# Cross-attention and quantised feed-forward on one core: the shape of the reads, of the first loads and of the warm-up

## The chip, the cores and the metric

The kernel runs on one core of a Trainium2 chip. The metric is the device time of one execution in microseconds (us). A core has five engines with a queue of instructions each: TensorE (PE in the profile, its weight loads PEld), VectorE (DVE), ScalarE (ACT), GpSimd (POOL) and SyncE (SP). SyncE computes nothing here; it issues DMAs. DMAs issued by SyncE, ScalarE and GpSimd are carried out by 16 DMA engines that the queues share.

## The reference

`x` and `ctx` are 4 x 1024 x 512 floats. Normalisation, biases and all weights are as below; the attention has 16 heads of 32, and a mask by blocks: 768 image tokens attend within three chunks of 256, and 256 text tokens attend to all image tokens and causally to text.

```python
qh = heads(layernorm(x) @ Wq + bq); kh = heads(ctx @ Wk + bk); vh = heads(ctx @ Wv + bv)
scores = where(mask, einsum('bhqd,bhkd->bhqk', qh, kh) * 32 ** -0.5, -inf)
x = x + merge(softmax(scores) @ vh) @ Wo + bo

xq = fake_quant(layernorm(x), clip_x)            # one scale for the whole tensor, 8 bits
gate, up = xq @ fq(w_gate).T, xq @ fq(w_up).T    # 512 -> 1408, weights by rows, 8 bits
h = fake_quant(silu(gate) * up, clip_down)
x = x + h @ fq(w_down).T
```

## The kernel before

Tokens are cut into 16 blocks of 256 (`QB`), four to a batch element: three image blocks and one text block. Two kinds of job are done for each block: `kv` (its context turned so that features lie on partitions, then K and V) and `q` (normalised x turned, then Q). A large loop (L984) goes over *units*: an image block has 4 units, one for each group of four heads; a text block has 16, one for each group and each quarter of the keys. The order of units and jobs is written out by hand, and the order on PE, DVE, ACT and POOL is the order of the code (`manual_schedule`, L923). SyncE's queue alone is ordered by the scheduler of the framework.

**Image units of the first three batch elements (36 of them, `rows`)** compute their scores with queries on partitions. `maxima` (L456) makes scores and their maxima, `exponents` (L492) the exponentials E and their sums, `quotients` (L508) divides on GpSimd. The weights must then be turned so that keys lie on partitions. This goes through DRAM and VectorE: `send_out` (L514) stores E, 128 partitions of 8 KB, in a DRAM tile `e_d`; `fetch` (L519) reads it back into the tile `S` in another arrangement; `turned` (L525) transposes 32 x 32 blocks of S on VectorE (L530); `row_values` (L532) multiplies by V. In the iteration of unit n, the loop fetches unit n - 2 (L998), stores unit n - 1 (L1000), then issues the posts (among them the store of normalised x, L400), the loads for the next small step (`prepare_next`, L1003) and the load of x1 for an output (`xr`, L137 by way of L1008), and transposes unit n - 3 (L1012). E and S have two buffers each. A fetch is four DMAs of 256 KB: each fills 32 partitions, with four rows of 2 KB on each.

Other image units and all text units compute scores a second time with keys on partitions (`weights`, L581), and need no such turn. Image stages with the round trip through DRAM lie at about 45 to 211, 318 to 449 and 552 to 690 us.

**Contexts.** `load_spread` (L143) reads a context block so that one VectorE transpose by blocks (L280) turns it: for image blocks by `mixed=True`, eight DMAs, each with 32 partitions by 4 runs of 512 bytes; for text blocks and for normalised x four DMAs with 32 partitions by 8 runs. The first context block is loaded by `load_mixed` (L154) and turned on TensorE against the identity (L291), with copies out on ScalarE (L292).

**Start.** After 14 warm-up products (L174, 128 x 512 each) come the loads: first context block, Wk in four chunks by `ci` (L178, each 128 partitions by 512; two on SyncE's queue and two on ScalarE's), biases on ScalarE's queue, the first x block, then Wv and Wq in four DMAs each of 32 partitions by 4 rows (L185), all on SyncE's queue.

**Background.** `statistics`, `deviation`, `apply` normalise an x block, and `largest`, `quantise` quantise a feed-forward weight. They stand in a deque, of which each iteration takes one at L1026, and one more after a `quantise` (L1029). After attention, the feed-forward stage (from about 985 us) has its own loops (L1287, L1359).

Of the kernel before, what the change touches and what calls it, by code (L numbers as in the profile page):

```python
# [10 lines left out]
F32 = mybir.dt.float32  # L11
# [8 lines left out]
P = 128  # L20
B, N, C = 4, 1024, 512
NH, D = 16, 32
FF = 1408
NCC = C // P
NIC = FF // P
QB = 256
NQB = N // QB
# [15 lines left out]
def kernel(ctx: ExitStack, tc: tile.TileContext, x, kv, Wq, bq, Wk, bk, Wv, bv, Wo, bo, clip_x, clip_down, w_gate, w_up, w_down, out):  # L43
    nc = tc.nc
    x_tok = x.rearrange("b n c -> (b n) c")
    kv_tok = kv.rearrange("b n c -> (b n) c")
# [11 lines left out]
    ident = cpool.tile([P, P], F32, tag="ident", name="ident")  # L58
# [3 lines left out]
    ones = cpool.tile([P, P], F32, tag="ones", name="ones")  # L62
# [58 lines left out]
    with ExitStack() as actx:  # L121
# [20 lines left out]

        def load_spread(src, c, mixed=False):  # L143
            t = ld.tile([P, NQB * 2, P], F32, tag="cb", name=f"spread_{c}")
            for i in range(NCC):
                to, cols = t[i * D : (i + 1) * D], slice(i * P, (i + 1) * P)
                if not mixed:
                    nc.sync.dma_start(to, src[:, cols].rearrange("(k q) m -> q k m", q=D))
                    continue
                for n in range(2):  # L150
                    nc.sync.dma_start(to[:, n * 4 : (n + 1) * 4], src[:, cols].rearrange("(g n q) m -> n q g m", n=2, q=D)[n])
            return t

        def load_mixed(src, c):  # L154
            t = ld.tile([P, 2, C], F32, tag="cb", name=f"cb_{c}")
            for g in range(4):
                rows = src[c * QB + g * 2 * D : c * QB + (g + 1) * 2 * D, :]
                nc.sync.dma_start(t[g * D : (g + 1) * D], rows.rearrange("(n q) c -> q n c", q=D))
            return t

        brow = ap.tile([3 * NCC, P], F32, tag="brow", name="brow")
# [9 lines left out]

        idle = ps_mm.tile([P, 512], F32, tag="mm", name="idle")
        rhs = onesb.unsqueeze(1).to_broadcast([P, 4, P])
        for _ in range(14):  # L174
            nc.tensor.matmul(idle.rearrange("p (a b) -> p a b", a=4), onesb, rhs, start=True, stop=True)
        cb0 = load_mixed(kv_tok, 0)
        for ci in range(NCC):
            (nc.sync if ci % 2 == 0 else nc.scalar).dma_start(W["Wk"][:, ci, :], Wk.rearrange("(i k e) f -> k i e f", k=NCC, e=D)[ci])  # L178
        for i, bias in enumerate((bq, bk, bv)):
            nc.scalar.dma_start(brow[i * NCC : (i + 1) * NCC, :], bias.rearrange("(c p) -> c p", p=P))  # L180
        nc.scalar.preload_act_table_set("natural_log_exp_and_others")
        xb0 = load_block(x_tok, 0, "xb")
        for name, w in (("Wv", Wv), ("Wq", Wq)):
            for i in range(NCC):
                nc.sync.dma_start(W[name][i * D : (i + 1) * D], w[i * P : (i + 1) * P, :].rearrange("(k e) f -> e k f", e=D))  # L185

        def other_loads():
            nc.sync.dma_start(W["Wo"], Wo.rearrange("(c p) f -> p c f", p=P))
# [40 lines left out]


        Q, K, V = {}, {}, {}
        xbs, spreads = {0: xb0}, {}

        early = [True]

# [28 lines left out]
        class Job:  # L264


            def __init__(self, kind, c, a):
                self.kind, self.c, self.a = kind, c, a
                self.small, self.big, self.part = 0, 0, 0
                self.smalls = 2 if c == 0 else 1  # L270
                self.bigs = 4 if kind == "kv" else 2

            def run_small(self):
                if self.small == 0:
                    self.T = wk2.tile([P, NCC, QB], F32, tag="tT", name=f"{self.kind}T_{self.c}")
                i = self.small
                self.small += 1
                if self.c > 0:
# [4 lines left out]
                if self.kind == "q":  # L283
                    while not ready.get(self.c):
                        background.popleft()()
                src = cb0 if self.kind == "kv" else xb0
# [6 lines left out]
                if i == 1 and self.kind == "kv":  # L293
                    columns_of_biases()
                elif i == 1:
                    next_queries(self.c)

            def rows(self, dst, w, b, scale, co, parts):
# [215 lines left out]
        def send_out(u):  # L514

            u.through = dram.tile([P, 8 * QB], F32, tag="e_d", name=f"e_d_{u.n}", bufs=4)
            nc.sync.dma_start(u.through, u.e.rearrange("p g n h x k -> p (g n h x k)"))

        def fetch(u):  # L519

            u.spread = t = bp.tile([P, 4, 2, QB], F32, tag="S", name=f"S_{u.n}")
            for g in range(4):
                nc.sync.dma_start(t[g * D : (g + 1) * D].rearrange("p b n f -> p b (n f)"), u.through.rearrange("(b q) (g f) -> g q b f", q=D, g=4)[g])

        def turned(u):  # L525

# [282 lines left out]
        def small_step():  # L809
            nonlocal at_small  # L810
            jobs[at_small].run_small()
            if jobs[at_small].small == jobs[at_small].smalls:
                at_small += 1
# [145 lines left out]
                posts.popleft()()  # L959

        small_step()
        small_step()
        send(2)
        take = jobs[0].first_rows()
        stage()
# [18 lines left out]
        for n in range(len(units) + V_LAG):  # L984
# [450 lines left out]
```

## Time and profile before

| | us |
|---|---|
| median of 3 runs | 1268.04 (1264.88 to 1270.05) |
| the profiled execution | 1271.16 |
| its span in the profile | 1269.3 |
| PE busy | 1112.7 (88%) |
| DVE busy | 788.8 (62%) |
| ACT busy | 558.7 (44%) |
| POOL busy | 539.1 (42%) |
| moved by DMA | 214.72 MB, 158832 packets |

Times in the profile count from the span's start. In the slices of a page, each digit is the busy share of one fortieth of the span, in tenths. The DMA share is the mean over the 16 engines, so 0.25 is four engines busy all the time, or sixteen for a quarter of it. A line such as "L523 SPq" is the queue of SyncE at line 523, and "to landing" runs from the issue of a DMA to the completion that others wait for. Engines wait on semaphores in the order of their queue: a waiting instruction holds everything behind it on its engine.

### The profile page before, as it was taken

To read this page: it belongs to the slowest core of one execution; us is meant where nothing else is said; L and a number is where in the kernel's file an instruction comes from. 1 tells how busy PE (TensorE), PEld (TensorE's weight loads), DVE (VectorE), ACT (ScalarE), POOL (GpSimd) and SP (SyncE) were. 2 spreads that over 40 slices of the span, in tenths; PEclk is the share of its full clock that TensorE was granted. 3 is DMA by queue.
4 is the path that set the end of the run, shared out by engine and by line. 5 is a ranking of instruction groups with operands and counts; after the bars stand their busy time and mean duration, and the time that the engine had idled before them with its cause. 6 is when DMAs were issued, how large, how long until landed. Compare 5 with 4: busy or idle time off the path is not lost.

```text
span 1269.3 us, 30483 instructions
## 1 busy us (share of the span) xinstructions
PE 1112.7 (88%) x12891; PEld 534.4 (42%) x12891; DVE 788.8 (62%) x1086; ACT 558.7 (44%) x1205; POOL 539.1 (42%) x542
## 2 busy tenths in 40 slices
PE   6977486989989798998988899999989894999898
PEld 4533232444443334454333445555544442344344
DVE  0435456745467784645678565585666784687797
ACT  1555241335754323486351344453434452544453
POOL 1334240468954316887351486675662221100010
PEclk7998697989999997998999999999989898899899
DMA  6599789945798962559798654211311399520595
GB/s 149 176 263 237 221 230 270 260 97 92 242 242 235 277 161 50 121 176 255 215 255 243 153 102 104 73 49 55 118 41 57 115 263 185 105 58 17 215 383 206
DMA packets 158832, 214.72 MB, mean 169 GB/s; under 512 B 49756, under 2 KB 99944, under 8 KB 152680
## 3 DMA queue, kind: packets, MB, share of 16 engines
q1 hardware_dynamic: 136200, 170.83, 49.5%
q0 software_dynamic: 22208, 41.42, 12.7%
q8 instruction: 101, 1.65, 0.6%
q10 hardware_dynamic: 288, 0.53, 0.1%
q14 instruction: 35, 0.29, 0.1%
HBM read 120.59 MB, written 90.70 MB: 166 GB/s over the span
## 4 chain that ended last, share of the span: by engine, by line
PE 37%; DVE 6%; DMA 5%; POOL 3%; issue 2%; ACT 2%; SPq 0%; DVEq 0%; POOLq 0%; ACTq 0%
PE pg L1275 5%; PE pu L1275 5%; PE pd L1378 4%; PE po L239 4%; PE pv L239 3%; PE av L642 3%; PE pp_q L239 2%; PE t L595 2%; PE s L479 2%; POOL sp L621 2%; DMA wdT<-wdq 2%; DMA xqT<-xq 2%; PE pp_kv L239 1%; PE s L468 1%; PE av L661 1%
## 5 line engine op out<-in xcount | busy, mean ns | idle before, releaser
L621 POOL TENSOR_TENSOR sp<-sp,pT 128x1024 f32<-128x1024 f32 x84 | 188.9, 2249 | 43.2 <-ACT pT L604 39.9
L512 POOL TENSOR_TENSOR E<-E,sums 128x1024 f32<-128x1024 f32 x72 | 135.7, 1893 | 153.0 <-DVE sums L510 105.6
L490 DVE TENSOR_REDUCE nmh<-s 128x2 f32<-128x1024 f32 (+1 forms) x128 | 145.1, 1155 | 56.1 <-PE s L479 53.9
L499 ACT ACTIVATE E<-s,nmh 128x256 f32<-128x256 f32 x288 | 132.7, 481 | 86.1 <-DVE nmh L472 37.0
L472 DVE TENSOR_REDUCE nmh<-s 128x4 f32<-128x1024 f32 x96 | 112.6, 1214 | 87.9 <-PE s L468 87.9
L600 ACT ACTIVATE pT<-t 128x1024 f32<-128x1024 f32 x76 | 78.0, 1027 | 200.3 <-PE t L595 196.8
L239 PE MATMUL pp_kv<-kvT,Wk_sb 128*32 128x256 f32 x1920 | 119.5, 400 | 18.3 <-DVE xr L695 18.1
L239 PE MATMUL pv<-Wv_sb,kvT 128*32 128x512 f32 (+1 forms) x1088 | 123.0, 587 | 4.8 <-DMA spread_kv<-in_ctx_dram 3.4
L239 PE MATMUL po<-Wo_sb,oT 128*32 128x512 f32 (+1 forms) x1056 | 114.4, 573 | 10.4 <-DVE xr L695 9.0
L239 PE MATMUL pp_q<-qT,Wq_sb 128*32 128x256 f32 x2048 | 121.9, 388 | 0.0
L1275 PE MATMUL pg<-xqT,wgT 128*128 128x512 bf16 x352 | 92.8, 388 | 21.2 <-DMA xqT<-xq 20.4
L1302 DVE SCALAR_TENSOR_TENSOR h<-pu,su,silu 128x512 f32<-128x512 f32 x88 | 65.4, 747 | 54.4 <-PE pu L1275 53.4
L1281 ACT ACTIVATE silu<-pg,sg 128x512 f32<-128x512 f32 x88 | 59.9, 686 | 89.0 <-PE pg L1275 89.0
L543 PE MATMUL av<-pT,va 128*32 128x256 f32 x576 | 48.4, 427 | 50.6 <-DVE pT L530 37.8
L1275 PE MATMUL pu<-xqT,wuT 128*128 128x512 bf16 x352 | 92.3, 386 | 0.0
L239 PEld LDWEIGHTS pp_kv<-kvT,Wk_sb 128*32 128x32 f32 x1920 | 62.4, 115 | 68.8 <-DVE xr L695 18.5
L530 DVE STREAM_TRANSPOSE pT<-S 128x1024 f32<-128x1024 f32 x72 | 85.0, 1218 | 6.2 <-DMA S<-e_d 6.2
L239 PEld LDWEIGHTS pp_q<-qT,Wq_sb 128*32 128x32 f32 x2048 | 64.5, 112 | 52.7 <-issue 9.8
L642 PE MATMUL av<-pT,va 128*32 128x256 f32 (+1 forms) x1216 | 80.5, 376 | 6.3 <-POOL pT L609 5.5
L479 PE MATMUL s<-kT,qT 32*128 32x256 f32 (+1 forms) x1024 | 82.2, 405 | 4.1 <-ACT pT L600 2.5
L595 PE MATMUL t<-qT,kT 32*128 32x256 f32 (+1 forms) x1216 | 80.4, 377 | 0.0
L604 ACT ACTIVATE pT<-t 128x1024 f32<-128x1024 f32 x76 | 78.0, 1027 | 0.0
(198 smaller groups left out, 1590.5 us busy)
## 6 DMA issues: line engine op xcount, KB each, us to landing
e_d<-E SPq DMA_DIRECT2D x36, 1024.0 KB, 5.9
S<-e_d SPq DMA_DIRECT2D x144, 256.0 KB, 6.4
xt<-x_d SPq DMA_DIRECT2D x16, 1024.0 KB, 8.0
h<-h_d POOLq DMA_DIRECT2D x3, 2816.0 KB, 13.4
xb<-in_x_dram SPq DMA_DIRECT2D x16, 512.0 KB, 7.6
x_d<-bo_b SPq DMA_DIRECT2D x16, 512.0 KB, 9.1
x_d<-in_x_dram POOLq DMA_DIRECT2D x16, 512.0 KB, 7.6
xr<-x_d SPq DMA_DIRECT2D x16, 512.0 KB, 5.2
```

Source lines behind the costliest of these rows:

```text
L239: nc.tensor.matmul(out[rows_of(j)], lhs[:, rows_of(j)], rhs, start=start, stop=stop, tile_position=(0, j * D), skip_group_check=True)
L472: nc.vector.tensor_reduce(nmh[:, h, :, :, 0], prs[h], AX.X, ALU.max, negate=True)
L479: nc.tensor.matmul(prs[j // 2][:, j % 2, kk, :w], q[rows_of(j), g, i * P : (i + 1) * P], K[k.keys[2 * half + kk]][rows_of(j), g, :w], star ...
L490: nc.vector.tensor_reduce(nmh[:, h, :, i, half], s[:, :, :n], AX.X, ALU.max, negate=True)
L499: nc.scalar.activation(u.e[:, :, :, h, x, :].rearrange("p g n k -> p n g k"), u.s[h][:, jj, i, :].rearrange("p (n g k) -> p n g k", n=2, g=4),
L512: nc.gpsimd.tensor_tensor(e, e, u.sums[h].unsqueeze(1).unsqueeze(3).to_broadcast([P, 8, 4, D]), ALU.mult)
L530: nc.vector.transpose(pT[:, n], u.spread[:, :, n].rearrange("p b (y k) -> p b y k", k=D))
L595: nc.tensor.matmul(prs[j // 2][:, j % 2, n, cols], kc[rows_of(j), g, n * P : (n + 1) * P], q[rows_of(j), g, cols], start=False, stop=(n == 1))
L600: nc.scalar.activation(pT[:, :2], prs[0], AF.Exp)
L621: nc.gpsimd.tensor_tensor(sp[:, :, cols], a, pT[:, :, n, cols], ALU.add)
L642: nc.tensor.matmul(av[rows_of(j), 0, cols], va[:, n, g * P + j * D : g * P + (j + 1) * D], u.pT[:, j, n, cols], start=(u.part == 0 and n = ...
L1275: nc.tensor.matmul(ps, w[:, ic, cc, :], qT[:, cc, :], start=(cc == 0), stop=(cc == NCC - 1))
```

## The change

1. `fetch` reads S in four DMAs by b in place of four by g. Each still has 128 rows of 2 KB; it fills all 128 partitions with one row each, where it was 32 partitions with four rows each.
2. `load_spread(mixed=True)` likewise: eight DMAs of 128 partitions with one run of 512 bytes. The first context block is now loaded by it and turned by VectorE like the others; `load_mixed`, its products and its copies are gone, and `columns_of_biases` is called from the start of the schedule.
3. Wk comes in four chunks on ScalarE's queue; Wv and Wq in four chunks each, in turn on SyncE's and ScalarE's queues, all in the form that Wk had.
4. The warm-up has 10 of the large products, and then 7 rounds of 16 small ones on 32 x 32 tiles (256 columns in four rounds, 64 in three).
5. In the loop, `send_out` comes after the posts, `prepare_next` and the load of x1.
6. One more background step is taken in an iteration when it is `statistics` or `largest`, and more wait.

SyncE's queue, as the scheduler orders it, changes with this: where it sometimes had two stores of E in a row and then two fetches, store and fetch now alternate nearly everywhere, and in the first image stage the load of the next x block stands ahead of that of x1.

```diff
         def load_spread(src, c, mixed=False):
             t = ld.tile([P, NQB * 2, P], F32, tag="cb", name=f"spread_{c}")
-            for i in range(NCC):
-                to, cols = t[i * D : (i + 1) * D], slice(i * P, (i + 1) * P)
-                if not mixed:
-                    nc.sync.dma_start(to, src[:, cols].rearrange("(k q) m -> q k m", q=D))
-                    continue
-                for n in range(2):
-                    nc.sync.dma_start(to[:, n * 4 : (n + 1) * 4], src[:, cols].rearrange("(g n q) m -> n q g m", n=2, q=D)[n])
+            if mixed:
+                for k in range(NQB * 2):
+                    n, g = k // 4, k % 4
+                    at = (2 * g + n) * D
+                    nc.sync.dma_start(t[:, k], src[at : at + D, :].rearrange("q (i m) -> i q m", i=NCC))
+            else:
+                for i in range(NCC):
+                    nc.sync.dma_start(t[i * D : (i + 1) * D], src[:, i * P : (i + 1) * P].rearrange("(k q) m -> q k m", q=D))
...
-        for _ in range(14):
+        for _ in range(10):
             nc.tensor.matmul(idle.rearrange("p (a b) -> p a b", a=4), onesb, rhs, start=True, stop=True)
-        cb0 = load_mixed(kv_tok, 0)
-        for ci in range(NCC):
-            (nc.sync if ci % 2 == 0 else nc.scalar).dma_start(W["Wk"][:, ci, :], Wk.rearrange("(i k e) f -> k i e f", k=NCC, e=D)[ci])
+        tiles = [ps_sc.tile([P, 2, 2, QB], F32, tag="sc", name=f"idle_{h}") for h in range(2)]
+        for rounds, n in ((4, QB), (3, 2 * D)):
+            for _ in range(rounds):
+                for k in range(4):
+                    for j in range(4):
+                        nc.tensor.matmul(
+                            tiles[j // 2][k * D : (k + 1) * D, j % 2, 0, :n].rearrange("p (a b) -> p a b", b=2 * D),
+                            ident[j * D : (j + 1) * D, k * D : (k + 1) * D],
+                            ones[j * D : (j + 1) * D, : 2 * D].unsqueeze(1).to_broadcast([D, n // (2 * D), 2 * D]),
...
+        def load_weight(name, w, queues):
+            for ci in range(NCC):
+                queues[ci % len(queues)].dma_start(W[name][:, ci, :], w.rearrange("(i k e) f -> k i e f", k=NCC, e=D)[ci])
+
+        first = {0: load_spread(kv_tok[:QB, :], "kv_0", True)}
+        load_weight("Wk", Wk, [nc.scalar])
...
-        for name, w in (("Wv", Wv), ("Wq", Wq)):
-            for i in range(NCC):
-                nc.sync.dma_start(W[name][i * D : (i + 1) * D], w[i * P : (i + 1) * P, :].rearrange("(k e) f -> e k f", e=D))
+        load_weight("Wv", Wv, [nc.sync, nc.scalar])
+        load_weight("Wq", Wq, [nc.sync, nc.scalar])
...
             u.spread = t = bp.tile([P, 4, 2, QB], F32, tag="S", name=f"S_{u.n}")
-            for g in range(4):
-                nc.sync.dma_start(t[g * D : (g + 1) * D].rearrange("p b n f -> p b (n f)"), u.through.rearrange("(b q) (g f) -> g q b f", q=D, g=4)[g])
+            for b in range(4):
+                nc.sync.dma_start(t[:, b].rearrange("p n f -> p (n f)"), u.through.rearrange("(b q) (g f) -> b g q f", q=D, g=4)[b])
...
                 fetch(before)
-            if previous is not None and previous.rows:
-                send_out(previous)
             for post in [posts.popleft() for _ in range(len(posts))]:
                 post()
             prepare_next(n)
...
                         o.load()
+            if previous is not None and previous.rows:
+                send_out(previous)
...
+            extra = background.popleft() if f is not None and len(background) > 1 and background[0].__name__ in ("statistics", "largest") else None
...
-            if f is not None:
-                f()
+            for stage_ in (f, extra):
+                if stage_ is not None:
+                    stage_()
```

More of the change, by code (lines that the diff above doesn't have):

```diff
@@ L144, in load_spread @@
             t = ld.tile([P, NQB * 2, P], F32, tag="cb", name=f"spread_{c}")
-            for i in range(NCC):
-                to, cols = t[i * D : (i + 1) * D], slice(i * P, (i + 1) * P)
-                if not mixed:
-                    nc.sync.dma_start(to, src[:, cols].rearrange("(k q) m -> q k m", q=D))
-                    continue
-                for n in range(2):
-                    nc.sync.dma_start(to[:, n * 4 : (n + 1) * 4], src[:, cols].rearrange("(g n q) m -> n q g m", n=2, q=D)[n])
-            return t
-        def load_mixed(src, c):
-            t = ld.tile([P, 2, C], F32, tag="cb", name=f"cb_{c}")
-            for g in range(4):
-                rows = src[c * QB + g * 2 * D : c * QB + (g + 1) * 2 * D, :]
-                nc.sync.dma_start(t[g * D : (g + 1) * D], rows.rearrange("(n q) c -> q n c", q=D))
+            if mixed:
[6 more added lines that the diff above has]
+                    nc.sync.dma_start(t[i * D : (i + 1) * D], src[:, i * P : (i + 1) * P].rearrange("(k q) m -> q k m", q=D))
             return t
@@ L173 @@
         rhs = onesb.unsqueeze(1).to_broadcast([P, 4, P])
-        for _ in range(14):
+        for _ in range(10):
             nc.tensor.matmul(idle.rearrange("p (a b) -> p a b", a=4), onesb, rhs, start=True, stop=True)
-        cb0 = load_mixed(kv_tok, 0)
-        for ci in range(NCC):
-            (nc.sync if ci % 2 == 0 else nc.scalar).dma_start(W["Wk"][:, ci, :], Wk.rearrange("(i k e) f -> k i e f", k=NCC, e=D)[ci])
+        tiles = [ps_sc.tile([P, 2, 2, QB], F32, tag="sc", name=f"idle_{h}") for h in range(2)]
[7 more added lines that the diff above has]
+                            ones[j * D : (j + 1) * D, : 2 * D].unsqueeze(1).to_broadcast([D, n // (2 * D), 2 * D]),
+                            start=True,
+                            stop=True,
+                            tile_position=(j * D, k * D),
+                            skip_group_check=True,
+                        )
+        def load_weight(name, w, queues):
[3 more added lines that the diff above has]
+        load_weight("Wk", Wk, [nc.scalar])
         for i, bias in enumerate((bq, bk, bv)):
@@ L231 @@
         Q, K, V = {}, {}, {}
-        xbs, spreads = {0: xb0}, {}
+        xbs, spreads = {0: xb0}, first
         early = [True]
@@ L269, in __init__ @@
                 self.small, self.big, self.part = 0, 0, 0
-                self.smalls = 2 if c == 0 else 1
+                self.smalls = 2 if c == 0 and kind == "q" else 1
                 self.bigs = 4 if kind == "kv" else 2
@@ L277, in run_small @@
                 self.small += 1
-                if self.c > 0:
+                if self.c > 0 or self.kind == "kv":
                     src = spreads.pop(self.a)
@@ L281, in run_small @@
                     return
-                if self.kind == "q":
+                if True:
                     while not ready.get(self.c):
                         background.popleft()()
-                src = cb0 if self.kind == "kv" else xb0
+                src = xb0
                 pt = bank(f"pt_{self.kind}_{self.c}_{i}").rearrange("p (a b) -> p a b", a=NCC)
@@ L292, in run_small @@
                 nc.scalar.copy(self.T[:, :, i * P : (i + 1) * P], pt)
-                if i == 1 and self.kind == "kv":
-                    columns_of_biases()
-                elif i == 1:
+                if i == 1:
                     next_queries(self.c)
@@ L521, in fetch @@
             u.spread = t = bp.tile([P, 4, 2, QB], F32, tag="S", name=f"S_{u.n}")
-            for g in range(4):
-                nc.sync.dma_start(t[g * D : (g + 1) * D].rearrange("p b n f -> p b (n f)"), u.through.rearrange("(b q) (g f) -> g q b f", q=D, g=4)[g])
+            for b in range(4):
+                nc.sync.dma_start(t[:, b].rearrange("p n f -> p (n f)"), u.through.rearrange("(b q) (g f) -> b g q f", q=D, g=4)[b])
         def turned(u):
@@ L961 @@
         small_step()
-        small_step()
+        columns_of_biases()
         send(2)
```

## The prediction

> **What bounds the kernel now.** I read the page's slices first, for where the DMA engines are full; then windows over the three stretches in which image units run; then windows over the first 21 us, where both shapes of load stand apart; then the queue totals; then the two lines that store E and fetch S; last SyncE's timeline in one image stage.
>
> From the page, busy time, slices and one queue (slices are 31.7 us):
>
> ```profile
> PE 1112.7 (88%) x12891; PEld 534.4 (42%) x12891; DVE 788.8 (62%) x1086; ACT 558.7 (44%) x1205; POOL 539.1 (42%) x542
> ...
> DMA  6599789945798962559798654211311399520595
> GB/s 149 176 263 237 221 230 270 260 97 92 242 242 235 277 161 50 121 176 255 215 255 243 153 102 104 73 49 55 118 41 57 115 263 185 105 58 17 215 383 206
> ...
> q10 hardware_dynamic: 288, 0.53, 0.1%
> ```
>
> TensorE is the busiest, but in slices 2 to 6, 11 to 13 and 18 to 21 the DMA engines reach 8 or 9 tenths at only 220 to 277 GB/s, while slice 39 moves 383 GB/s. Those are the stages in which the image units' weights go through DRAM (E stored, S fetched). Windows over them (after PE, PEld, DVE, ACT and POOL: granted clock, DMA share, GB/s):
>
> ```profile
> 45.00:211.00 166.00, 117.30 (x1546) 52.06 (x1546) 82.88 (x120) 69.96 (x253) 55.87 (x52) 0.86 0.85 239
> 345.00:445.00 100.00, 83.98 (x1104) 35.98 (x1100) 68.97 (x96) 44.40 (x161) 45.65 (x36) 0.97 0.93 251
> 570.00:690.00 120.00, 104.13 (x1316) 45.25 (x1314) 81.32 (x112) 54.12 (x188) 54.25 (x40) 0.93 0.89 242
> ```
>
> No compute engine is as full there as DMA: 85, 93 and 89%. The image stages have no room for dearer transfers. What the two shapes cost is seen at the start:
>
> ```profile
> 5.00:7.00 2.00, 1.11 (x6) 0.29 (x3) 0.00 (x0) 0.20 (x1) 0.00 (x0) 1.00 0.26 96
> 9.00:11.00 2.00, 0.00 (x0) 0.00 (x0) 0.00 (x0) 0.00 (x0) 0.00 (x0) 0.50 0.26 97
> 16.00:21.00 5.00, 5.00 (x24) 4.08 (x23) 0.00 (x0) 0.00 (x0) 0.00 (x0) 1.00 1.07 187
> ```
>
> In the first two, chunks of Wk load (L178, 128 partitions by 512 elements, 256 KB each). With several outstanding on two queues only 0.26 of 16 engines, about four, are busy, at 97 GB/s: 24.2 GB/s for each. In the third, Wv and Wq load by L185 (32 partitions by 4 by 512): all 16 engines are busy, but at 187 GB/s, 11 GB/s each. The 32-partition form stretches its packets; the 128-partition form runs them at full pace on a quarter of the engines. The line of q10 (ScalarE's queue) says it again: two chunks of 128 rows and three biases of 4 rows make 268 packets of data; the other 20 are completions, four for each of five transfers.
>
> The two lines of the round trip, and SyncE in the second image stage:
>
> ```profile
> L523 SPq DMA_DIRECT2D S<-e_d x144: 302/430/1864, 60.0 to 677.9; - x144
> ...
> DMA to landing us min/median/max: 3.3/6.4/9.7
> ```
>
> ```profile
> L517 SPq DMA_DIRECT2D e_d<-E x36: 320/338/891, 54.5 to 668.4; - x36
> ...
> DMA to landing us min/median/max: 4.2/5.9/9.2
> ```
>
> ```profile
> 382.96 0.34 SPq L517 DMA_DIRECT2D e_d<-E  x1
> ...
> 391.61 0.35 SPq L517 DMA_DIRECT2D e_d<-E  x1
> 392.08 4.20 SPq L523 DMA_DIRECT2D S<-e_d  x4
> ...
> 400.98 1.73 SPq L523 DMA_DIRECT2D S<-e_d  x4
> 405.70 0.34 SPq L517 DMA_DIRECT2D e_d<-E  x1
> ```
>
> 36 units each store 1 MB and fetch it back in four reads. By SyncE's issues the twelve stores of a stage run from 54.5 to 185.5, 318.3 to 432.3 and 552.0 to 668.4 us: 11 intervals of 131, 114 and 116 us, so 11.9, 10.4 and 10.6 us a unit.
>
> **The change part by part.**
>
> *The S fetch.* Count, bytes and row length stay (4 reads of 128 rows of 2 KB). The source, written (g q) f, now begins with g = 4 and the target with 128 partitions: exactly the shape of a Wk chunk, whose row is therefore the nearest. Each read goes over four engines, and as chunks outstanding together kept 0.26 busy, I take the same four for all reads. Each then carries 262 KB a unit: 262/24.2 = 10.8 us. Now a fetch takes every engine 4.8 us (512 packets over 16 engines at 150 ns, the packet records' median between 345 and 445 us).
>
> The Trainium skill speaks on both sides. "Trainium Kernel Development and Optimization", section Best Practices, says to tile always to 128 partitions; by that alone a fetch would run on 16 engines, 65.5/24.2 = 2.7 us, and the sum would be rival B. "DMA: Bandwidth & Descriptors", section "Why a DMA increments its semaphore by 16 and not by 1", says that the engines are the largest number up to 16 that divides the outermost size of both sides, here 4 and 128, and that this queue takes the lowest-numbered ones; by that the sum is mine. The Wk rows decide for the second.
>
> *Load of one of the four engines, a unit.* Besides S: the E store over 16 engines, 65.5/24.2 = 2.7 us. The rest from the windows: 0.85 x 166 = 141 us for 12 fetches, 0.93 x 100 = 93 for 10, 0.89 x 120 = 107 for 10; less 4.8 for each fetch and 2.7 for each store leaves 4.2, 1.8 and 3.2 us a unit (x, xn, x1, weights). The context loads take the same shape (8 reads, 512-byte rows, 27 ns a packet): 256 packets x 27 = 6.9 us on four engines in place of 1.7 on all; three such in the first stage and one in each other: 1.3, 0.5, 0.5 us a unit. Sums: 19.0, 15.8 and 17.2 us.
>
> *The chain.* On SyncE the changed order is store n+1, fetch n+1, store n+2 in strict turn for nearly all units. Fetch n+1 waits for store n+1, whose part on the four engines stands behind fetch n. So a unit is at least 10.8 + 2.7 + 1.5 us, the last from landing to SyncE's next first packet (0.4 from the last packet of the store at 143.4 to its landing, 1.1 from the issue at 60.0 to the first packet). That is 15.0 with no other traffic, and with all of it in line 20.5, 17.3 and 18.7. The load gives 19.0, 15.8, 17.2; half the 1.5 us gap will not be filled, so I take 19.8, 16.5, 18.0. Times 11: 218 + 182 + 198 = 598 us against 361: **+237**. The median slack between S landing and its transpose (L530) is some 9 us; that hides one late fetch, not a rate.
>
> *Store behind posts, prepared loads and xr (L1006 to L1016).* It puts xb's load ahead of the store. In the first stage VectorE waits 32.9 us for xb and SyncE 22.1 us over the run for x1's accumulation (ahead of xr). With the four engines full the gain is covered by them: 0. Bounds -33 and +22; the store and its fetch now stand behind xr's wait.
>
> *Start.* The four engines carry context 6.9, Wk, Wv and Wq 10.8 each, x 1.4: 40.7 us from the first packet at 1.8 us, so Wq lands at some 43 to 44 us. The query products now start at 37.8; the first finds its last chunk 6 us later: **+6**. Bounds -3 (two products fewer before it) and +10. The 32 KB bias loads' queue place, the transpose that moves from TensorE to VectorE, and the warm-up (4 of 14 products of 0.36 us out, 112 small ones in; 64 transposes on 32 columns, two passes each, took 3.6 us, so some 6 to 10) lie under these loads: 0, at worst +2 if the warm-up outlasts the context.
>
> *One more background step an iteration.* Statistics and weight maxima come earlier on VectorE, 62% busy; no count changes. 0; at most ±5, since TensorE is 283 of 295 us busy between 690 and 985 and cannot use it.
>
> Sum: the profiled execution took 1271.2 us (span 1269.3), 0.25% above the median of 1268.0. 1271 + 237 + 6 = 1514, on the median's scale **1510 us**.
>
> **Rivals.**
> A. The same, and SyncE's waits in line add up: the 22.1 us for x1 repeat with slower landings (+22), start +10, chain at its full 20.5, 17.3, 18.7 (+20): some 1560. For it: SyncE issues in order. Against: most loads are due well ahead.
> B. Other side, faster: reads of 128 partitions spread over all 16 engines. A fetch falls from 4.8 to 2.7 us, the 32.9 us wait for xb goes: 1268 - 33 = 1235. It decides if a fetch occupies more than about seven engines, since 1 MB must pass within the 4.8 us of now beside the store. For it: stretched packets do vanish. Against: 0.26 and 20 completions.
> C. Only the chain binds: other traffic falls into its gaps, 15.0 a unit: 495 - 361 = +134, so 1400. Against: the load alone is above it in every stage.
> D. Hidden: four engines, but S is needed late: 1268. The slack must grow every unit; it can't, since 15 is over 10.6.
>
> **How the numbers follow.** Forecast 0.62, A 0.15, B 0.08, C 0.12, D 0.03. Range 1410 to 1590: from just above C to past A; B, D and half of C are out. A measurement of this kernel tells 0.5% (6 us) from no change; faster 0.08, same 0.02, slower 0.90.
>
> **What the profile after would show.** Right: in the image stages GB/s falls to some 150 to 170 and DMA share to about 0.5, with S fetches landing after 11 us and more; VectorE's wait for S before L530 (6.2 us in all) becomes the longest wait; stores 16 to 20 us apart; text and feed-forward stages unchanged. At the start, share 0.26 to 0.4 until 40 us. Wrong: S landing within 6 us and share of 0.8 there would be B. The forecast fails if Wk's four engines are due to something other than its shape.

## The result: 1511 us, and where the 240 us lie

| | us |
|---|---|
| before, median of 4 runs | 1268.21 (1264.88 to 1270.05) |
| after, median of 4 runs | 1510.77 (1505.47 to 1517.22) |
| ratio after / before | 1.1918, 95% interval 1.1864 to 1.1973 |
| span in the profile, before and after | 1269.3 and 1507.3 |

The change makes the kernel slower by 19%. The kernel before has two levels, and all its runs in this table are on the upper one, while in the experiments (on three chips) most of its runs lie between 1234 and 1254 us, with a few at 1258 to 1272 that the comparisons leave out; there the whole change measures 1.2188 (1.2131 to 1.2245).

From the page of the kernel after, busy time, slices (now of 37.7 us) and the queue of ScalarE:

```profile
PE 1174.4 (78%) x13025; PEld 550.2 (36%) x13047; DVE 794.8 (53%) x1087; ACT 556.6 (37%) x1203; POOL 540.5 (36%) x542
...
DMA  2435666574445434453553444745201314971386
GB/s 102 156 142 174 183 197 228 160 188 94 101 151 143 149 143 160 146 117 82 143 150 137 157 147 171 169 115 101 79 15 38 109 41 139 269 199 29 110 328 239
...
q10 hardware_dynamic: 1080, 2.10, 0.4%
```

The compute engines are busy for about as long as before (TensorE 62 us longer, at a lower granted clock in the image stages), but each for a smaller share of the time. In the image stages, DMA shares of 8 and 9 tenths are gone, and the rate is 137 to 197 GB/s, with 228 in one slice, where it was 220 to 277. Windows over the three image stages say it with sharper edges (after PE, PEld, DVE, ACT and POOL: granted clock, DMA share, GB/s):

```profile
66.00:276.00 210.00, 126.51 (x1402) 50.29 (x1398) 76.34 (x109) 63.19 (x231) 51.44 (x48) 0.78 0.55 183
405.00:609.00 204.00, 131.03 (x1476) 55.56 (x1468) 79.66 (x111) 67.46 (x228) 70.96 (x57) 0.79 0.46 149
732.00:933.00 201.00, 133.82 (x1478) 56.11 (x1468) 79.67 (x111) 67.47 (x228) 71.03 (x57) 0.79 0.47 152
```

Share and rate fall together, from 0.85 to 0.93 at 239 to 251 GB/s. On the mean, fewer of the 16 engines work at a time. The queue of ScalarE counts them again: eight weight chunks of 128 rows and three biases of 4 rows are 1036 packets; the other 44 are four completions for each of 11 transfers.

SyncE's own waits show what it now stands for. First of the kernel before, then of the kernel after (us in total, times, longest):

```profile
SPq L517 <- POOL E L512: 106.1, 28, 8.8
...
SPq L523 <- DMA e_d<-E: 71.0, 19, 8.6
```

```profile
SPq L531 <- DMA e_d<-E: 230.6, 27, 13.5
```

Before, a store mostly waited for its data to be computed (106 us). After, that wait is not among the longest nine, and the fetch waits for the store to land, 231 us in all. So computing no longer sets the pace; the round trip does. The compute engines see it as follows (the first lines of the waits of the kernel after):

```profile
POOL E L520 <- DVE sums L518: 325.1, 56, 18.6
...
PE av L551 <- DVE pT L538: 191.6, 32, 25.9
ACT E L507 <- DMA e_d<-E: 176.7, 18, 15.5
...
DVE pT L538 <- DMA S<-e_d: 100.0, 20, 8.1
```

VectorE waits 100 us for S before its transposes. ScalarE waits more, 177 us: E has two buffers, and a buffer comes free when its store lands. Others wait for these two in turn. SyncE in one stage:

```profile
562.63 2.66 SPq L531 DMA_DIRECT2D S<-e_d  x4
565.39 2.17 SPq L525 DMA_DIRECT2D e_d<-E  x1
...
579.78 2.57 SPq L531 DMA_DIRECT2D S<-e_d  x4
582.45 0.62 SPq L525 DMA_DIRECT2D e_d<-E  x1
...
596.02 2.57 SPq L531 DMA_DIRECT2D S<-e_d  x4
```

Fetch, store, fetch, store in strict turn, 16 to 17 us a unit here. From first to last store a stage takes 209.5, 203.1 and 200.4 us (66.0 to 275.5, 405.4 to 608.5, 732.5 to 932.9), together 613 where it was 361.

The ledger of the two profiled executions: the first store comes 11.5 us later; the three stages take 78.5, 89.1 and 84.0 us more; what lies between them -2.9 and +4.3; what follows the last store 574.4 in place of 600.9 us, -26.5. Sum +238, the difference of the spans. The last term is the gate and up products of the feed-forward stage, from 188 us (996.3 to 1184.8) to 163 us (1259.4 to 1423.0). At their line TensorE sat idle before for 20.4 us until the activations were loaded, and after never for that reason (idle time of that line until its releaser, first before, then after):

```profile
  issue: 30.0, 32
  DMA xqT<-xq: 20.4, 2
```

```profile
  issue: 3.7, 13
```

No part of the change touches that stage, and in the profiles of the other kernels shown below, the kernel before with one part of the change among them, it takes 163 to 166 us. So the 25 us belong to the execution of the kernel before shown here, not to the change. What held that execution up there was not tried.

### The profile page after: what moved, and what is told of

Read it like the earlier page. It is cut to its first block, busy times and chain, and to the rows that moved or that the text cites. A ratio compares the mean times of both kernels' runs of the same rounds, so it can differ in the third digit from the quotient of the medians.

```text
span 1507.3 us, 30793 instructions
## 1 busy us (share of the span) xinstructions
PE 1174.4 (78%) x13025; PEld 550.2 (36%) x13047; DVE 794.8 (53%) x1087; ACT 556.6 (37%) x1203; POOL 540.5 (36%) x542
## 3 DMA queue, kind: packets, MB, share of 16 engines
q0 software_dynamic: 22208, 41.42, 10.5%
## 4 chain that ended last, share of the span: by engine, by line
PE 37%; DMA 30%; SPq 12%; POOL 7%; DVE 5%; ACT 4%; issue 3%; DVEq 0%; ACTq 0%; POOLq 0%
DMA e_d<-E 13%; DMA S<-e_d 7%; PE pg L1285 5%; PE pu L1285 5%; SPq L149 4%; POOL sp L629 4%; PE pd L1388 4%; SPq L152 4%; PE pv L249 3%; SPq L531 3%; DMA xn_d<-xb 3%; PE av L650 3%; PE t L603 3%; PE s L487 3%; PE po L249 2%
## 5 line engine op out<-in xcount | busy, mean ns | idle before, releaser
L520 POOL TENSOR_TENSOR E<-E,sums 128x1024 f32<-128x1024 f32 x72 | 136.0, 1893 | 330.5 <-DVE sums L518 325.1
L507 ACT ACTIVATE E<-s,nmh 128x256 f32<-128x256 f32 x288 | 133.3, 487 | 261.8 <-DMA e_d<-E 176.7
L551 PE MATMUL av<-pT,va 128*32 128x256 f32 x576 | 66.7, 568 | 201.7 <-DVE pT L538 191.6
L608 ACT ACTIVATE pT<-t 128x1024 f32<-128x1024 f32 x76 | 78.0, 1026 | 201.4 <-PE t L603 194.7
L249 PE MATMUL po<-Wo_sb,oT 128*32 128x512 f32 (+1 forms) x1056 | 126.7, 624 | 20.6 <-ACT va L366 13.1
L249 PE MATMUL pp_kv<-kvT,Wk_sb 128*32 128x256 f32 x1920 | 123.9, 411 | 20.4 <-DVE xr L703 14.5
L249 PE MATMUL pp_q<-qT,Wq_sb 128*32 128x256 f32 x2048 | 130.6, 408 | 2.7 <-ACT va L366 1.9
L551 PEld LDWEIGHTS av<-pT,va 128*32 128x32 f32 x576 | 16.2, 135 | 246.4 <-issue 165.7
L476 PE MATMUL s<-kT,qT 32*128 32x256 f32 x768 | 75.6, 448 | 7.5 <-ACT E L507 4.7
```

Source lines behind the costliest of these rows:

```text
L249: nc.tensor.matmul(out[rows_of(j)], lhs[:, rows_of(j)], rhs, start=start, stop=stop, tile_position=(0, j * D), skip_group_check=True)
L507: nc.scalar.activation(u.e[:, :, :, h, x, :].rearrange("p g n k -> p n g k"), u.s[h][:, jj, i, :].rearrange("p (n g k) -> p n g k", n=2, g=4),
L520: nc.gpsimd.tensor_tensor(e, e, u.sums[h].unsqueeze(1).unsqueeze(3).to_broadcast([P, 8, 4, D]), ALU.mult)
L551: nc.tensor.matmul(av[rows_of(j)], va[:, n, g * P + j * D : g * P + (j + 1) * D], pT[:, j // 2, n, j % 2, :], start=(n == 0), stop=(n == 1 ...
```

## The experiments

All are measured against the kernel before on the same chip, whose median was 1244 to 1246 us there; a ratio of 1.01 is thus 12.4 us. Every kernel computes the whole reference.

### The fetch alone, and all but the fetch

The kernel before with the new fetch and nothing else:

```diff
-            for g in range(4):
-                nc.sync.dma_start(t[g * D : (g + 1) * D].rearrange("p b n f -> p b (n f)"), u.through.rearrange("(b q) (g f) -> g q b f", q=D, g=4)[g])
+            for b in range(4):
+                nc.sync.dma_start(t[:, b].rearrange("p n f -> p (n f)"), u.through.rearrange("(b q) (g f) -> b g q f", q=D, g=4)[b])
```

> The kernel before with the fetch of S by b alone (128 partitions, four reads). Theory: units at 17 to 20 us as in the changed kernel, 1268 + 220 to 245 = 1490 to 1515 us, stores 16 to 20 us apart. Rival (order of the queue, or start and contexts, carry most): under 1400 us.

The kernel after with the same four lines the other way round, so that all else of the change stays:

> The changed kernel with the four reads of S by g again (32 partitions each), all else changed. Theory (the fetch on four engines makes the unit): the image units return to 10.5 to 12 us, and what is left is the context reads on four engines and the start: 1268 + 6 for the start + up to 15 for the contexts - up to 33 for xb = 1250 to 1290 us, 1275 the likeliest. Rival (the order of the queue, store behind posts and loads, makes it slow): still above 1400 us.

Fetch alone: 1476.94 us, 1.1826 (1.1701 to 1.1951), some 227 us more, as the first expectation has it. All but the fetch: 1263.54 us, 1.0144 (1.0045 to 1.0243), within the second one's 1250 to 1290 us. The fetch carries more than nine tenths of the loss, some 227 of 272 us (0.1826 of 0.2188, times 1244); the rest costs some 18 us by itself.

The profile of the kernel with the new fetch alone is the place to see what sets the pace, since contexts, weights and order are the old ones. SyncE in its second stage:

```profile
439.45 2.46 SPq L523 DMA_DIRECT2D S<-e_d  x4
441.95 2.08 SPq L517 DMA_DIRECT2D e_d<-E  x1
...
456.32 2.45 SPq L523 DMA_DIRECT2D S<-e_d  x4
458.87 2.10 SPq L517 DMA_DIRECT2D e_d<-E  x1
```

The packet records between the two fetches: the 512 packets of the first run from 440.79 to 453.31 us, four at a time on the mean, 98 ns each. Three quarters of the store's 128 packets of 8 KB, which go to the other twelve engines, are through by 449.90. The last 32 start as the fetch runs out and end at 455.77. The next fetch's first packet is at 457.66. So a unit is 12.5 + 2.5 + 1.9 = 16.9 us. Other transfers seem to come into it only as far as they stretch the fetch's packets, from the 84 ns of the median to 98 on the mean. Its stores lie 17.1, 17.2 and 16.9 us apart in the three stages (188.3, 188.7 and 186.0 over 11). But the first stores of a stage go ahead of their fetches, so this is a little too low: VectorE's transposes of S, which come last in the round trip, lie 18.1, 17.9 and 17.6 us apart. In the second and third stage the fetches follow each other in 16.2 to 22.5 us, with a median of 17.4, so the unit taken apart here is typical. In the first they vary from 5.5 to 31.5 us, and the equal mean there does not show that the same chain sets it.

### Half of the fetch

Two of the four blocks are read in the new form, the other two in the old one:

```diff
-            for g in range(4):
-                nc.sync.dma_start(t[g * D : (g + 1) * D].rearrange("p b n f -> p b (n f)"), u.through.rearrange("(b q) (g f) -> g q b f", q=D, g=4)[g])
+            for b in range(2):
+                nc.sync.dma_start(t[:, b].rearrange("p n f -> p (n f)"), u.through.rearrange("(b q) (g f) -> b g q f", q=D, g=4)[b])
+            for g in range(4):
+                nc.sync.dma_start(t[g * D : (g + 1) * D, 2:].rearrange("p b n f -> p b (n f)"), u.through[2 * D :, :].rearrange("(b q) (g f) -> g q b f", q=D, g=4)[g])
```

> The kernel before; blocks 0 and 1 of S are read by b in two 128-partition reads, blocks 2 and 3 by g in four 32-partition reads of half the bytes. Theory (rate of the four engines): a unit's load on them is 5.4 + 2.4 + 2.7 + others = 14.7, 12.3 and 13.7 us in the three stages against 11.9, 10.4 and 10.6 now: + 86, so 1350 us. Rival (cost in proportion to the reads on four engines): half of the full fetch's cost, 1380 to 1390. Rival (late landing, hidden up to the slack of 9 us): 1268 to 1275, as S lands some 3 us later only.

1316.24 us, 1.0602 (1.0520 to 1.0684), some +75 us, below both sums and nearer to the smaller one. That is a third of the whole fetch's 227, not half of it, so the loss doesn't grow in proportion to the bytes that go over four engines. That the first part of a longer round trip goes into slack which the kernel before has fits this, but the slack itself was not measured. The stages took 156.7, 138.4 and 132.9 us from first to last store, and the share stands between the two kernels (0.70, 0.70 and 0.69 in windows over them).

### The store on another queue

The new fetch alone, and the store of E issued by GpSimd, so that it no longer stands behind a fetch in SyncE's queue. Beside it, the same step in the kernel before.

```diff
-            nc.sync.dma_start(u.through, u.e.rearrange("p g n h x k -> p (g n h x k)"))
+            nc.gpsimd.dma_start(u.through, u.e.rearrange("p g n h x k -> p (g n h x k)"))
```

> The kernel before with the new fetch, and the store of E issued by GpSimd, so that on the four engines it no longer stands behind the fetch in one queue. With the new fetch alone the units took 17.1, 17.2 and 16.9 us in the three stages. Theory (chain in the second and third stage, load in the first): units 17, 15 and 16 us, some 35 us less than the new fetch alone, ratio 1.15 to 1.16. Rival (the chain alone binds): 15 us in all stages, 60 us less, ratio 1.13. Rival (the load of the four engines alone): no change, 1.18.

> The kernel before with the store of E issued by GpSimd and the fetch as it was: beside e9 it tells what the other queue does by itself. SyncE waits 106 us in all for E before its stores; 0.985 to 1.005 of before.

With the new fetch: 1446.75 us, 1.1626 (1.1561 to 1.1691), so 0.020 less than with the store on SyncE's queue. In the kernel before: 1242.11 us, 0.9989 (0.9954 to 1.0024), nothing. The stores are no measure of the unit here: by them the three stages are 66 us shorter, by the span all is 34 us shorter (1437.4 for 1471.4). VectorE's transposes of S are one. In the second stage, the first and the last pair of them with the store on SyncE's queue, then with the store on GpSimd's:

```profile
396.57 2.37 DVE L530 STREAM_TRANSPOSE pT<-S 128x1024 f32<-128x1024 f32 x2 [0.18 <-DMA S<-e_d]
...
593.10 2.37 DVE L530 STREAM_TRANSPOSE pT<-S 128x1024 f32<-128x1024 f32 x2 [8.65 <-DMA S<-e_d]
```

```profile
407.47 2.37 DVE L530 STREAM_TRANSPOSE pT<-S 128x1024 f32<-128x1024 f32 x2 [5.63 <-DMA S<-e_d]
...
579.78 2.37 DVE L530 STREAM_TRANSPOSE pT<-S 128x1024 f32<-128x1024 f32 x2 [3.15 <-DMA S<-e_d]
```

Over 11 intervals a unit took 18.1, 17.9 and 17.6 us in the three stages, and now takes 18.3, 15.7 and 15.8: nothing less in the first, 2.2 and 1.9 us less in the second and third, near the 2.5 us that the store's last packets took behind the fetch. This is the part of the chain that the queue's order makes. What is left is near what each of the four engines must carry for S and E: 128 packets at 94 ns (the mean from 420 to 540 us) and 8 at 312 ns (the median there) are 12.0 + 2.5 = 14.5 us. So in the second and third stage the chain was the bound, and the load lay some 2 us below it. In the first stage the queue's order is not what binds. These are about the units of the theory, 17, 15 and 16 us, and its ratio, 1.15 to 1.16, is touched by the interval; that the load binds in the first stage fits, but was not shown.

### 128 partitions on 16 engines

Can the fetch fill 128 partitions and still go over all engines? It can if E lies in DRAM in the order in which it is fetched. Then the store takes the 32-partition shape instead:

```diff
-            nc.sync.dma_start(u.through, u.e.rearrange("p g n h x k -> p (g n h x k)"))
+            for b in range(4):
+                to = u.through[b * D : (b + 1) * D, :].rearrange("p (r f) -> (p r) f", f=2 * QB).rearrange("(g q) f -> q g f", g=4)
+                nc.sync.dma_start(to, u.e[b * D : (b + 1) * D].rearrange("p g n h x k -> p g (n h x k)"))
...
-            for g in range(4):
-                nc.sync.dma_start(t[g * D : (g + 1) * D].rearrange("p b n f -> p b (n f)"), u.through.rearrange("(b q) (g f) -> g q b f", q=D, g=4)[g])
+            nc.sync.dma_start(t.rearrange("p b n f -> p b (n f)"), u.through.rearrange("(b s) (r f) -> b (s r) f", b=4, f=2 * QB).rearrange("b p f -> p b f"))
```

> The kernel before with E stored in the order in which it is fetched: four stores of 32 partitions by 4 runs of 2 KB, and one fetch of 128 partitions by 4 rows of 2 KB, whose outer size is 128 on both sides. Theory (the outer sizes set the number of engines, 32-partition writes stretch the packets): the fetch runs on 16 engines unstretched, 2.7 us of each in place of 4.8, and the DMA share in the image stages falls; time 0.97 to 1.00 of before, 0.985 the likeliest, as the stages wait for more than DMA. If reads of 32 partitions stretch as well: 1.00. Rival (128-partition reads are slow as such): 1.15 and more.

1257.74 us, 1.0107 (1.0080 to 1.0134). The fetch is one DMA of 128 partitions with four rows each. It lands 6.7 us after its issue on the median (the trace has the landing of 7 of the 36), where in the kernel with the new fetch alone the packets by themselves took 12.5 us:

```profile
L524 SPq DMA_DIRECT2D S<-e_d x36: 360/376/1358, 62.5 to 686.8; - x36
...
DMA to landing us min/median/max: 5.6/6.7/9.5
```

Where one can be seen by itself (issued at 385.6 us, with the stores behind it) its 512 packets all start between 386.6 and 390.2 us, at a median of 84 ns. Reading over four engines is the slow part. But nothing is won either, although the packets take less time. From 345 to 445 us 62% of all 2 KB packets took over 120 ns before, and 13% do here. The stores, now from 32 partitions, are stretched in part: from 411.8 to 413.2 us, where the first of four runs by itself, its packets take 153 ns on the median, but those that stand behind the fetch in the queue, from 417.4 to 420.4 us, take 84. The DMA share falls with it, in that window from 0.93:

```profile
345.00:445.00 100.00, 85.20 (x1072) 35.53 (x1072) 64.16 (x91) 47.76 (x172) 49.99 (x37) 0.95 0.83 252
```

So reads that fill 128 partitions are not slow as such, and the lower share that I expected came without the gain in time. Why it is 1.1% slower was not followed further.

### Contexts, order and start

By its stores the changed kernel has 18.2 to 19.0 us a unit, the fetch alone 16.9 to 17.2; by the transposes it is 18.4 to 19.1 and 17.6 to 18.1. What makes the difference? Four kernels take one other part each, two of them on top of the new fetch. First the loop's image contexts in the new form, without and with the new fetch:

```diff
-            for i in range(NCC):
-                to, cols = t[i * D : (i + 1) * D], slice(i * P, (i + 1) * P)
-                if not mixed:
...
+            if mixed:
+                for k in range(NQB * 2):
+                    n, g = k // 4, k % 4
+                    at = (2 * g + n) * D
+                    nc.sync.dma_start(t[:, k], src[at : at + D, :].rearrange("q (i m) -> i q m", i=NCC))
```

> The kernel before with the loop's image contexts in the new form alone (eight reads of 128 partitions by one run of 512 bytes). Theory (each context holds four of the sixteen engines 5.2 us longer, 6.9 against 1.7, in stages with the DMA engines 0.85 to 0.93 busy, so part of it shows): 1.005 to 1.012, as is left of 1.0144 of the changed kernel with the old fetch when the start is taken off. Rival (contexts are due well ahead, and the fetches that stand beside them go over sixteen engines and fit in between): 0.997 to 1.002.

> The kernel before with the new fetch and the loop's image contexts in the new form. With the new fetch alone 1.1826 was measured on this scale, 17.1 us a unit in every stage. Theory 1 (the same four engines serve both, and a context's 6.9 us stand in the line of a fetch): five contexts by 5.2 us, +26 us on 1245, so 1.200 to 1.207. Theory 2 (the chain of store and fetch leaves the four engines idle for some 2 us a unit, in which a context goes): 1.180 to 1.188. The whole change measured 1.2188 there; less the start's 0.004 to 0.007 it leaves 1.212 to 1.215 for what fetch, contexts and order do together.

Then the order (the store behind the posts, the prepared loads and the load of x1) and the additional background step, without and with the new fetch:

```diff
-            if previous is not None and previous.rows:
-                send_out(previous)
             for post in [posts.popleft() for _ in range(len(posts))]:
...
                         o.load()
+            if previous is not None and previous.rows:
+                send_out(previous)
```

> The kernel before with only the store of E behind the posts, prepared loads and xr, and the extra background step. Theory: both are small; VectorE's 32.9 us wait for xb in the first image stage shrinks, a store behind xr's wait costs up to 22: 1240 to 1280 us, 1258 the likeliest. Rival (the order makes the changed kernel slow): above 1350 us.

> The kernel before with the new fetch, the store of E behind the posts, the prepared loads and the load of x1, and the additional background step. New fetch alone: 1.1826. Order and background alone: 1.0023. Theory 1 (store and fetch in strict turn is the chain that I reckoned with, and it stands in the kernel with the new fetch alone too): 1.180 to 1.188. Theory 2 (a store that stands behind SyncE's wait for x1 comes later, and with the chain as the bound each such delay shows, 22 us over the run in the profile of before): 1.195 to 1.202. If this and the run with the contexts both stay below 1.19, the 1.5 us a unit that the whole change has more come from the two together.

Last the start: weights in chunks on two queues, the first context in the new form, the new warm-up. Fetch, order and the loop's contexts are the old ones.

> The kernel before with the start of the change alone: Wk, Wv and Wq in four chunks each over two queues, the first context block in the new form and turned by VectorE, the new warm-up. The fetch, the order, the background and the context loads of the loop stay as before. Theory (the four engines carry context, Wk, Wv, Wq and x, 40.7 us by my sum, and the query products wait for Wq): +5 to +8 us, ratio 1.004 to 1.007, first store later by about as much. Rival (the first store, which came 11.5 us later in the changed kernel, is late through the start alone): ratio 1.008 to 1.010. Rival (the start is hidden by work that is done later anyway): within 0.998 to 1.002.

And the whole change again, on one of these chips:

> The changed kernel once more, on the chip of the runs beside it, since the kernel before took 1268 us where the changed one was first measured and 1246 us elsewhere: 1.18 to 1.20 of the kernel before. The new fetch alone gave 1.183, all but the fetch 1.014; if the two simply add, 1.197.

| part | with the old fetch | with the new fetch |
|---|---|---|
| fetch | | 1.1826 (1.1701 to 1.1951) |
| contexts | 1.0041 (0.9998 to 1.0084) | 1.2034 (1.1955 to 1.2114) |
| order and background | 1.0023 (0.9985 to 1.0060) | 1.1892 (1.1813 to 1.1972) |
| start | 1.0085 (1.0055 to 1.0114) | |
| whole change | 1.0144 (1.0045 to 1.0243) | 1.2188 (1.2131 to 1.2245) |

The whole change, at 1.2188, lies above the 1.18 to 1.20 that I expected on this chip: the fetch and the rest, 0.1826 and 0.0144, do not simply add. The contexts alone fall between their two expectations and decide nothing; on top of the new fetch they give 1.2034, theory 1, the line of the same four engines. The order on top of it lies just above theory 1, and its interval touches both.

With the new fetch the contexts add 0.0208, some 26 us, and the order 0.0066, some 8 us; by itself the context form adds 5 us, not clear of zero. Taken each in the kernel in which they stand, the parts add up. Old fetch: 0.0041 + 0.0023 + 0.0085 = 0.0149, measured 0.0144. New fetch: 0.1826 + 0.0208 + 0.0066 + 0.0085 = 0.2185, measured 0.2188. That agreement is closer than the intervals warrant. What is shown, if barely, is that the contexts cost time with the new fetch (the interval of the two together begins at 1.1955, that of the fetch alone, of three runs, ends at 1.1951); the profiled executions differ by 12.8 us (1484.2 for 1471.4), half of the 26. That the order costs anything is not shown.

Stores are a poor measure of these parts. From first to last store the three stages take 563.0 us with the fetch alone, 580.0 with the contexts added and 591.9 with the order added. But of the order's 28.9 us the span shows 7.5 (1478.9 for 1471.4): the stretches between the stages, 132.6 and 132.1 us, become 128.7 and 126.4, and what follows the last store 577.0 in place of 588.7. The transposes of S keep closer to the span: from the first to the last of a stage, 589.7 us in all with the fetch alone, 602.0 with the contexts and 600.8 with the order.

The start measures +10.6 us (6.8 to 14.2), which is the rival's 1.008 to 1.010, though the interval reaches into the theory's range as well. The first store decides: it comes at 66.4 us in this kernel, at 66.0 in the kernel after and at 54.5 before, so all of that delay is the start's. VectorE's timeline in this kernel, around the first unit, shows why:

```profile
46.06 1.25 DVE L301 STREAM_TRANSPOSE kvT<-spread_kv 128x1024 f32<-128x1024 f32 x1 [20.96 <-DMA spread_kv<-in_ctx_dram]
53.56 0.70 DVE L399 BATCH_NORM_STATS2 st<-xb 128x6 f32<-128x512 f32 x1 [6.25 <-DMA xb<-in_x_dram]
...
55.18 2.32 DVE L491 TENSOR_REDUCE nmh<-s 128x4 f32<-128x1024 f32 x2
```

The first maxima (L491) stand behind the statistics of the second x block (L399), which wait for its load until 53.5 us. In the kernel before the same statistics ran at 39.3 us and the maxima at 46.0. The load is late because SyncE could not issue it. SyncE's timeline, first of the kernel before, then of the kernel after:

```profile
22.92 7.66 SPq L151 DMA_DIRECT2D spread_kv<-in_ctx_dram  x8
34.67 0.39 SPq L137 DMA_DIRECT2D xb<-in_x_dram  x1
```

```profile
25.23 19.61 SPq L149 DMA_DIRECT2D spread_kv<-in_ctx_dram  x8
...
47.44 0.37 SPq L137 DMA_DIRECT2D xb<-in_x_dram  x1
```

Eight issues took 7.7 us before and 19.6 us after, while the weights ahead of them were still being moved by four engines; x's load went out 12.8 us later, and the first store came 11.5 us later.

## Why the prediction was right, and where its steps were not

**The bound, right.** Share and rate of the image stages fell as forecast (0.46 to 0.55 at 149 to 183 GB/s, forecast about 0.5 at 150 to 170), and stores lie 18.2 to 19.0 us apart, forecast 16 to 20. The landing of the fetches, forecast at 11 us and more, stands in no row of this trace; their packets alone took 12.5 us in the unit taken apart above.

**The S fetch on four engines, right; its time mis-sized.** The term was 10.8 us at the pace of a Wk chunk. With the new fetch alone it takes 12.5 us, at 98 ns a packet in place of 84. Rival B falls with it: a fetch that fills 128 partitions over 16 engines is fast (its packets started within 3.6 us in the experiment), but this one is not on 16 engines. Its bound of about seven engines was off: 1 MB in 4.8 us at 24.2 GB/s needs nine. The rule that the prediction set against rival B, in the Trainium skill's "DMA: Bandwidth & Descriptors", section "Why a DMA increments its semaphore by 16 and not by 1", agrees with three things here: four packets at a time in the fetch, four completions a transfer on ScalarE's queue, and the DMA of the experiment whose slowest size is 128 on the target and 128 in DRAM, which ran wide. It also says that transfers of this kind take the same lowest-numbered engines; with chunks on two queues at once, the window from 2 to 15 us has a share of 0.27 and 92 GB/s, and no more.

**Load or chain, wrong in two stages.** My working took the load of one of the four engines as the bound, 19.0, 15.8 and 17.2 us, and let the chain add half a gap. Without the new contexts that load would be 17.7, 15.3 and 16.7. The fetch alone gives 18.1, 17.9 and 17.6 by the transposes, and with the store on another queue 18.3, 15.7 and 15.8. So in the second and third stage the load is at most 15.7 and 15.8, and the chain, which I had put below it, is the bound. In the first stage, moving the store won nothing, and the load of 17.7 may well be right. The term that was too large is "the rest", in the third stage above all: beside the 14.5 us for S and E it can be 1.3 there at most, for 3.2, and 1.2 in the second, for 1.8. Packet times, from which I had it, do not add up to a load: with the store on another queue, S on four engines and a sixteenth of all other packets make 167 us from 390 to 540 us, in a window of 150. The chain, in turn, was too small at 15.0: it is 16.9 in the unit taken apart, from 12.5 for 10.8 in the fetch and 1.9 for 1.5 from landing to next packet; the store's share, 2.7, came out at 2.5. So rival C named the right mechanism for the second and third stage, and its number, 1400, fell short by the size of that chain and by the contexts.

**The contexts, not refuted in size.** 1.3, 0.5 and 0.5 us a unit are 25 us over the three stages; measured are some 26 with the new fetch, but by two runs' intervals that nearly touch, and 12.8 in the profiled executions. I had added them to a load. Two stages are bound by the chain instead, and that some of their time shows all the same says that the chain's idle time does not hide all of it.

**Load and chain together: 598 for the three stages, 613 measured.** By stage 218, 182 and 198 were forecast, and 209.5, 203.1 and 200.4 came: the first too much, the second, where the chain ruled, 21 us too little.

**Order and background, not told from the 0 that was taken.** It measures 0.0023 alone and 0.0066 with the new fetch, neither clear of zero. The reason that I gave fails: full engines were to cover the gain from an earlier xb, but the earlier issue gained next to nothing. VectorE's wait for xb between 45 and 290 us, 32.9 us before, is 28.2 with the order alone, and with the new fetch it grows, from 39.8 to 52.1. Rival A's +22 did not come: SyncE's wait for x1's accumulation, 22.1 us before, is 1.8 in the kernel after.

**Start, mis-sized.** +6 was forecast from Wq's landing, with +10 as the upper bound; the start alone measures +10.6. Wq did land as forecast, at 43.2 us, but I had charged only the query products. The step that I left out is the second x block behind SyncE's blocked issues, and the statistics that wait for it ahead of the first maxima on VectorE.

**The longest wait, wrong.** I named VectorE's wait for S. It grew from 6.2 to 100.0 us, but ScalarE's wait for a buffer of E is 176.7 us, and GpSimd's for the sums behind it 325.1. With E in two buffers, a late store stops the exponentials as well as the transposes.

**The sum.** 1271 + 237 + 6 came within a microsecond of the median, on its scale of 1510, by two misses that cancel: so close a number is luck. On the base of the experiments the change costs 0.2188 of 1244, or 272 us, and my terms came to 243. The image stages are the larger miss (fetch, contexts and order, 261 for 237), the start the smaller (10.6 for 6). The profile from which I counted was 25 us longer in the feed-forward stage than all others, which I had no way to see in a single one; "feed-forward unchanged" failed by just that.

## What to carry to other kernels

When a DMA's two sides are cut differently, look at the outermost size of both before counting partitions: filling 128 partitions from rows whose outermost size is four left four engines with the work of sixteen, and cost 18%. In a round trip through DRAM, count the chain (issue, packets on the busiest engine, the other transfer's packets queued behind them, landing) separately from the load, and put the queue's order into the chain. And a DMA share is not a load that can be carried over to another shape: packet times added up came to more than the window that they lay in. Last, measure a unit where the round trip ends; where it begins, work that goes ahead makes it look shorter.

## What was not expected

- A store spread over 16 engines waits for the four that the fetch keeps: 96 of its 128 packets were through at 449.9 us and the last 32 at 455.8, in the kernel with the new fetch alone. It lands as late as if all of it had been queued there.
- DMA issues themselves become slow when their engines are full. Eight issues of 128 rows each took 19.6 us on SyncE in the kernel after, 7.7 before; a store's single issue has a median of 1137 ns after, 338 before.
- Moving the 32-partition shape from the fetch to the store took most of the stretched packets away (62% of the 2 KB packets over 120 ns became 13% in the second image stage) and left the time 1.1% worse: the lower DMA share bought nothing.
- The biases, now issued behind all four of Wk's chunks on ScalarE's queue, hold TensorE: it sat idle for 10.5 us until they landed, and the granted clock between 15 and 30 us was 0.58, where it was 0.84 before. What that costs by itself was not separated from the late x block.
